# A graph layer on one core: two decoding matmuls for three, the negation and an absolute value on ScalarE, add and relu in one VectorE instruction

## The chip, the core and the metric

The kernel runs on one core of a Trainium2 chip. Its engines are TensorE (PE, with its weight loads as a row of their own, PEld), VectorE (DVE), ScalarE (ACT), GpSimd (POOL) and SyncE (SP); each works through its own queue in order, and they wait for one another by semaphores. The metric is the time of one execution on the device in microseconds (us).

## The reference

One layer of a graph network over N = 6250 nodes with D = 64 features and E = 206250 directed edges, sorted by their target:

```python
h = jnp.maximum(_layernorm(x, axis=-1), 0.0)
msg = jax.nn.relu(h[src] + edge_attr)
agg = jax.ops.segment_sum(msg, dst, num_segments=N)
t = h + agg
out = x + jax.nn.relu(t @ W1 + b1) @ W2 + b2
```

All of it is in float32. The costly part is `h[src]`: a row of 64 numbers for each of 206250 edges.

## The kernel before

**Tiling.** An edge group `g` is 768 edges: 128 partitions with G = 6 edges each. There are 268 groups and a rest. The first five are handled alone in the set-up; the others form KS = 150 sets `k` of one or two groups, and the main loop `for k in range(KS): both_units(k)` handles one set per turn. Its order of work is written out by hand in `both_units`, one half for odd and one for even `k`; generators (`picking`, `decoding`, `compared`, `counted`, `others`) are advanced a step at a time between the other calls, and each engine's queue holds its instructions in that order.

**Two ways to fetch a row of h.** Of a group's six edges per partition, three are gathered by POOL: `gather` (L241) issues an indirect DMA for each column of 128 edges, out of the copy of h in DRAM (`h_rows`) into `xg`. 114 of the sets have two groups and so six such gathers (the last fewer); 36 sets have one group and none. The other three are fetched with matmuls:

- `find` (L594) and `back` (L607): DVE compares lists of source nodes with numbers and writes one-hot matrices `found` and `backs` in float16.
- `across_of` (PE, `half`, L633) picks rows of h with `found`; ACT copies them to `across`; `turn_of` (PE, L644) transposes them into the one bank `turn`; `turn_out` (ACT) copies that to `picked` (L650); `pick` (PE, L655) puts them to the edges' places, and `decode_parts` (ACT, L720) copies the result to `both`.

**Two halves of a number.** A float16 matmul carries 11 bits, so the h of L633 is kept in `hp` as two float16 parts, `hi` and `lo`, scaled by UP = 2^12; the sign of `hi` carries one more bit, which says how the last place is to be corrected (`ln_parts`). After the pick, `decode_minus` (DVE) makes `minus = max(-both, 0)`. `decode_sum` (PE, L734) sums the parts into the PSUM bank `joint` with three matmuls for each of 6 columns of a set: `both` by `join`, `minus` by `weigh_sign` (it undoes the sign) and `minus` by `weigh_last` (the last place). `decode_add` (DVE, L743) adds the scaled sum to the edges' attributes in `ea`, `xg_add` (DVE, L750) adds the gathered rows to the other half of `ea`, and `messages` (ACT, L755) takes the relu of all of it in place.

**Sums.** `one_hot` (DVE, L696) marks for each edge its target in a window of 32 nodes; `window_sum` (PE, L769) multiplies messages by that mark, into `joint` as well, beside the decoded columns; `sum_into_z` (DVE, L687) adds the windows to `z`. At even `k` the windows of sets k-3 and k-2 are summed. Finished blocks of 512 nodes go through `hidden` and `result` and are stored.

**Pace of the gathers.** `passes` counts the nominal PE time of the matmuls as they are written; each time another SPREAD[0] ns (later SPREAD[1]) have been counted, it issues the next of 652 pending gathers, which waits for that matmul. The first 30 of the sets' gathers and 30 of the set-up's are issued ahead of that. `xgs` has room for ten sets, `eas` for four.

Of the kernel before, what the change touches and what calls it, by code (L numbers as in the profile page):

```python
# [9 lines left out]

F32 = mybir.dt.float32
I32 = mybir.dt.int32
I16 = mybir.dt.int16
F16 = mybir.dt.float16
AF = mybir.ActivationFunctionType
ALU = mybir.AluOpType
# [3 lines left out]
N, E, D = 6250, 206250, 64  # L20
P = 128
G = 6
# [19 lines left out]
H = 3  # L42
PP, RR = 128, 49
# [18 lines left out]
GROUPS = []  # L62
g = F0
# [6 lines left out]
KS = len(GROUPS)  # L70
# [6 lines left out]
QW = Q // VERSIONS  # L77
PLACED = [0, 2, 6, 22, 38, NCH]
RING, AHEAD, EAS = 10, 6, 4
SPREAD = 1110, 1190  # L80
UP, FINE = 2.0 ** 12, 2.0 ** 11
HALF_LAST = 2.0 ** -24 * (1 + 2.0 ** -9)
NUDGE, ODD = 0.12 * 2.0 ** -12, 0.35 * 2.0 ** -12
# [5 lines left out]
def kernel(  # L89
# [14 lines left out]
    nc = tc.nc  # L104
    ctx.enter_context(tc.manual_schedule())

    const = ctx.enter_context(tc.tile_pool(name="const", bufs=1))
    work = ctx.enter_context(tc.tile_pool(name="work", bufs=2))
# [14 lines left out]
    def x_rows(r, n):  # L123
        i = r // XH
        return xs[i][:, r - i * XH:r - i * XH + n]
# [34 lines left out]
    ident = lnp.tile([P, P], F32, name="ident", bufs=1)  # L160
# [13 lines left out]
    ones_b = const.tile([P, P], F16, name="ones_b")  # L174
    nc.vector.memset(ones_b, 1.0)
    join = const.tile([P, D], F16, name="join")
    weigh_sign = const.tile([P, D], F16, name="weigh_sign")
    weigh_last = const.tile([P, D], F16, name="weigh_last")
    nc.vector.scalar_tensor_tensor(join, ident[:, :D], FINE, ident[:, D:], op0=ALU.mult, op1=ALU.add)
    for t, by in ((weigh_sign, 2 * FINE), (weigh_last, -FINE * HALF_LAST)):  # L180
        nc.vector.tensor_scalar_mul(t, ident[:, :D], by)
    upper = const.tile([P, P], F16, name="upper")
    nc.gpsimd.affine_select(out=upper, in_=ones_b, compare_op=ALU.is_gt, fill=0.0, base=0,
                            pattern=[[1, P]], channel_multiplier=-1)
# [13 lines left out]
    hp = const.tile([PP, RR, 2, D], F16, name="hp")  # L198
# [8 lines left out]
    eas = [const.tile([P, 2, G, D], F32, name=f"ea{i}") for i in range(EAS)]  # L207
    xgs = [const.tile([P, 2, H, D], F32, name=f"xg{i}") for i in range(RING)]
    RAWS = (F0 + 1) // 2
# [37 lines left out]
    def first_col(g):  # L247
        return 0 if g < NG else G - CT

    def pool_cols(g):  # L250
        return G if g < F0 else 0 if g in WHOLE else G - H
# [20 lines left out]
    pending = [(g, j) for k in range(AHEAD, KS) for g in GROUPS[k] for j in range(first_col(g), pool_cols(g))]  # L272
    gates = [0, SPREAD[0]]
    current = []

    def passes(it, ns):
# [5 lines left out]
        if pending and gates[0] >= gates[1]:  # L282
            gates[1] += SPREAD[k >= 2 * SETS * SINGLES]
            assert k < set_of[pending[0][0]][0] < k + RING, (k, set_of[pending[0][0]][0], gates)
# [171 lines left out]
    joint = psum.tile([P, 512], F32, name="joint", bufs=1)  # L456
# [24 lines left out]
    def ln_rows(r, n, v):  # L481
        h = x_rows(r, n)
        nc.vector.reciprocal(v, v)
        nc.vector.tensor_scalar_mul(v, v, UP)
        nc.vector.scalar_tensor_tensor(h, h, 0.0, v.unsqueeze(2).to_broadcast([PP, n, D]),
                                       op0=ALU.max, op1=ALU.mult)
        nc.sync.dma_start(
            out=h_rows.rearrange("(p r) d -> p r d", r=RR)[:, r:r + n].rearrange("p r d -> p (r d)"),
            in_=h.rearrange("p r d -> p (r d)"),
        )  # L490
        return r, n, h
# [11 lines left out]
    def ln_turned():  # L503
        zv = z[:D, :NP].rearrange("d (p r) -> d p r", r=RR)
        for pt, r, n in turned_rows:
            nc.scalar.activation(zv[:, :, r:r + n], pt[:, :n].rearrange("d u p -> d p u"), AF.Copy, scale=1.0 / UP)
        turned_rows.clear()

    def ln_parts(r, m, h):
        hi, lo = hp[:, r:r + m, 0], hp[:, r:r + m, 1]  # L510
        rest = lnp.tile([PP, m, D], F32, name="rest")
        sign = lnp.tile([PP, m, D], F16, name="sign")
        nc.scalar.copy(hi, h)
        nc.scalar.mul(rest, h, FINE)
        yield
        nc.vector.scalar_tensor_tensor(rest, hi, -FINE, rest, op0=ALU.mult, op1=ALU.add)
        paces.append(nc.vector.scalar_tensor_tensor(lo, hi, NUDGE, rest, op0=ALU.mult, op1=ALU.add))
        yield
        nc.vector.tensor_tensor(rest, lo, rest, ALU.subtract)
        nc.vector.scalar_tensor_tensor(sign, hi, ODD, rest, op0=ALU.mult, op1=ALU.is_lt)  # L520
        yield
        nc.scalar.activation(sign, sign, AF.Copy, bias=1.0, scale=-2.0)
        yield
        nc.vector.tensor_tensor(hi, hi, sign, ALU.mult)

    def add_attr(y, xg, ea):
        nc.vector.scalar_tensor_tensor(y, xg, 1.0 / UP, ea, op0=ALU.mult, op1=ALU.add)

    def combine(xg, ea, n):
        add_attr(xg[:, :n], xg[:, :n], ea[:, :n])  # L530
        nc.scalar.activation(ea[:, :n], xg[:, :n], AF.Relu)
        return ea

    left = const.tile([P, CP], I16, name="left")
# [148 lines left out]
    aggs, hots, msgs = {}, {}, {}  # L683
# [20 lines left out]
    def first_messages(g):  # L704
        ea, xg = ring(eas, g), rows_of(g)
        if g < RAW:
            yield from norm_edges(xg)
            nc.vector.tensor_tensor(ea, ea, xg, ALU.add)
        else:
            add_attr(ea, xg, ea)  # L710
        nc.scalar.activation(ea, ea, AF.Relu)
        msgs[g] = ea
        yield

    fetched = {}
# [5 lines left out]

    def decode_minus(k):
        minus = work.tile([P, 2, H * P], F16, name="minus", bufs=1)
        nc.vector.tensor_scalar(minus, fetched[k], -1.0, 0.0, op0=ALU.mult, op1=ALU.max)  # L724
        fetched[k] = fetched[k], minus

    def decode_sum(k):
        both, minus = fetched.pop(k)
        for i in range(2):
            for j in range(H):  # L730
                to = joint[:, (i * H + j) * D:(i * H + j + 1) * D]
                terms = (both, join), (minus, weigh_sign), (minus, weigh_last)
                for n, (rows, weights) in enumerate(terms):
                    it = nc.tensor.matmul(to, rows[:, i, j * P:(j + 1) * P], weights, start=(n == 0), stop=(n == len(terms) - 1))  # L734
                    passes(it, 29)
                yield

    def decode_add(k):
        n = len(GROUPS[k])
        ea = eas[(k + RAWS) % EAS][:, :n]  # L740
        to = ea[:, :, G - H:] if n == 2 else ea[:, 0].rearrange("p (i j) d -> p i j d", i=2)
        to = to.rearrange("p i j d -> p i (j d)")
        nc.vector.scalar_tensor_tensor(to, joint[:, :2 * H * D].rearrange("p (i s) -> p i s", i=2),  # L743
                                       1.0 / (UP * FINE), to, op0=ALU.mult, op1=ALU.add)

    def xg_add(k):
        if len(GROUPS[k]) == 2:
            ea, xg = eas[(k + RAWS) % EAS], xgs[(k + RAWS) % RING]
            to = ea[:, :, :G - H].rearrange("p g j d -> p g (j d)")
            nc.vector.scalar_tensor_tensor(to, xg.rearrange("p g j d -> p g (j d)"), 1.0 / UP, to, op0=ALU.mult, op1=ALU.add)  # L750

    def messages(k):
        gs = GROUPS[k]
        msg = eas[(k + RAWS) % EAS][:, :len(gs)]
        nc.scalar.activation(msg, msg, AF.Relu)  # L755
        for i, g in enumerate(gs):
            msgs[g] = msg[:, i]

# [107 lines left out]
    def weave(*steps):  # L866

        steps = [step for step in steps if step is not None]
        while steps:
            steps = [step for step in steps if next(step, True) is None]  # L870
# [51 lines left out]
    def joined(k):  # L922
        yield from sums(k - 2)
        yield from sums(k - 1)
        yield from decode_sum(k)
# [3 lines left out]
            attr_set(k + EAS - 2)  # L929

    def joint_out(k):
        decode_add(k)
        yield
        if k > 0 and k % 2:
            yield from adds(k - 2)
            yield from adds(k - 1)
        one_hot(GROUPS[k])
        yield

    def both_units(k):  # L940
        current[:] = [k]
        d, odd = divmod(k, 2)
# [5 lines left out]
        if odd:  # L948
# [17 lines left out]
            next(compared, None)  # L966
            next(picking, None)
            turn_at(3 * k + 7)
            if k > 1:
                messages(k - 2)  # L970
            next(picking, None)
            across_at(3 * k + 9)
            counting(k, source, rank_turn)
# [6 lines left out]
            turn_at(3 * k + 8)  # L980
            next(decoding, None)
            next(decoding, None)
            weave(compared, counted, others)
            if not odd and d + 3 < KD:
                source_load(d + 3)
# [6 lines left out]
        else:  # L992
# [2 lines left out]
            next(compared, None)  # L995
            if k:
                decode_minus(k - 1)
            if k > 1:
                messages(k - 2)
            next(picking, None)  # L1000
            next(picking, None)
            counting(k - 1, rank_count)
# [27 lines left out]
            turn_at(3 * k + 8)  # L1030
            next(decoding, None)
            next(decoding, None)
            next(picking, None)
            if k:
                attrs_behind(k - 1)
# [43 lines left out]
    for r, to in quarters[2:]:  # L1079
        v = ln_var(*heads.pop(0))  # L1080
# [125 lines left out]
    any_left = nc.values_load(flag[0:1, 0:1], min_val=0, max_val=P * N)  # L1206
    xbs[NB] = old_rows(NB)
    decode_minus(KS - 1)
    messages(KS - 2)
    for k in (KS - 2, KS - 1):  # L1210
        for g in groups_of(k):
            starts_for(g)
    weave(joined(KS - 1))
    xg_add(KS - 1)
    weave(joint_out(KS - 1))
    messages(KS - 1)
    weave(sums(KS - 1))
    for g in range(KS - 4, KS - 1):
        behind.extend(groups_of(g))
# [30 lines left out]
    with tc.If(any_left > 0):  # L1250
        nc.gpsimd.iota(wide, pattern=[[1, WB]], base=1, channel_multiplier=0, allow_small_or_imprecise_dtypes=True)
        with tc.For_i(0, NG, 1) as i:
# [4 lines left out]
            ea = eas[0][:, 0]  # L1257
# [5 lines left out]
        ea = eas[0][:, 0]  # L1263
# [48 lines left out]
```

## Time and profile before

| | |
|---|---|
| median of 3 runs | 992.82 us (987.42 to 995.36) |
| the profiled execution | 989.2 us, of which 987.4 us from the first to the last instruction (the span) |
| granted TensorE clock, mean over the span | 0.968 of full speed |
| busy: PE, DVE, ACT, POOL | 905.7, 922.7, 780.2, 749.1 us |
| indirect gathers into xg | 682 |

A row of the groups names the line, engine, operation, what it writes and reads with the shapes, and the count; then the busy time in us and the mean of one in ns; then the idle time of the engine just before, with what ended most of it. A row of the timeline starts with the start and the duration in us, and its square bracket has the idle time ahead of the instruction and its releaser. The end of a matmul is modelled, so what one costs the queue is read from start to start.

### The profile page before, as it was taken

To read this page: it belongs to the slowest core of one execution; us is meant where nothing else is said; L and a number is where in the kernel's file an instruction comes from. 1 tells how busy PE (TensorE), PEld (TensorE's weight loads), DVE (VectorE), ACT (ScalarE), POOL (GpSimd) and SP (SyncE) were. 2 spreads that over 40 slices of the span, in tenths; PEclk is the share of its full clock that TensorE was granted. 3 is DMA by queue.
4 is the path that set the end of the run, shared out by engine and by line. 5 is a ranking of instruction groups with operands and counts; after the bars stand their busy time and mean duration, and the time that the engine had idled before them with its cause. 6 is when DMAs were issued, how large, how long until landed. Compare 5 with 4: busy or idle time off the path is not lost.

```text
span 987.4 us, 35954 instructions
## 1 busy us (share of the span) xinstructions
PE 905.7 (92%) x13996; PEld 728.2 (74%) x13996; DVE 922.7 (93%) x2314; ACT 780.2 (79%) x1623; POOL 749.1 (76%) x727
## 2 busy tenths in 40 slices
PE   2249999999999989999999999999999999999986
PEld 1137777878877778787887777887877787787874
DVE  8898999989999999999999899999999999999975
ACT  6528888878888878888888788887887888888873
POOL 7877777777777777777777777777777777777771
PEclk9559999999999999999999999999999999999998
DMA  7436667666766666776766766766766666676841
GB/s 222 140 100 196 192 230 232 208 226 210 217 218 210 216 216 205 223 240 217 225 215 205 227 215 212 261 202 202 243 214 212 223 217 228 214 234 208 272 146 36
DMA packets 93833, 205.63 MB, mean 208 GB/s; under 512 B 24537, under 2 KB 62042, under 8 KB 93658
## 3 DMA queue, kind: packets, MB, share of 16 engines
q1 hardware_dynamic: 70762, 179.87, 51.1%
q0 software_dynamic: 22784, 23.38, 12.8%
q8 instruction: 112, 1.84, 0.7%
q14 instruction: 63, 0.52, 0.2%
q10 hardware_dynamic: 112, 0.03, 0.0%
HBM read 199.07 MB, written 4.13 MB: 206 GB/s over the span
## 4 chain that ended last, share of the span: by engine, by line
PE 60%; DVE 19%; DMA 12%; issue 3%; ACT 3%; DVEq 1%; POOL 1%; SPq 0%; ACTq 0%; POOLq 0%
PE pick L655 19%; PE half L633 13%; DMA xg<-h_rows,src_sb 9%; PE joint L769 8%; PE turn L644 7%; DVE backs L611 6%; PE joint L734 6%; DMA sources<-source_row 2%; PE rows L432 2%; DVE ea L743 2%; DVE found L601 2%; ACT ea L755 2%; PE rows L366 1%; PE half L628 1%; PE rows L808 1%
## 5 line engine op out<-in xcount | busy, mean ns | idle before, releaser
L241 POOL DMA_INDIRECT xg<-h_rows,src_sb x682 | 711.5, 1043 | 207.9 <-issue 52.7
L655 PE MATMUL pick<-backs,picked 128*128 128x384 f16 x1800 | 437.4, 328 | 0.0
L650 ACT COPY picked<-turn 128x512 f16<-128x512 f16 x450 | 262.6, 584 | 69.2 <-PE turn L644 62.0
L639 ACT CAST across<-half 128x512 f16<-128x512 f32 x450 | 264.9, 589 | 18.6 <-PE half L633 10.5
L633 PE MATMUL half<-found,hp 128*128 128x128 f16 x3600 | 276.5, 220 | 0.0
L611 DVE TENSOR_SCALAR backs<-spots,ids 128x1536 f16<-128x1536 int16 x450 | 275.4, 647 | 0.0
L633 PEld LDWEIGHTS <-hp 128*128 128x128 f16 x3600 | 234.5, 98 | 37.9 <-issue 0.6
L601 DVE TENSOR_SCALAR found<-sources,nodes_of 128x1536 f16<-128x1536 int16 x300 | 191.8, 672 | 1.1 <-issue 0.8
L655 PEld LDWEIGHTS <-picked 128*128 128x128 f16 x1800 | 157.3, 99 | 34.0 <-issue 0.3
L644 PE MATMUL turn<-ident_h,across 128*128 128x128 f16 x1800 | 175.8, 220 | 1.7 <-ACT picked L650 1.7
L755 ACT ACTIVATE ea<-ea 128x768 f32<-128x768 f32 x150 | 115.6, 770 | 55.0 <-DVE ea L743 50.5
L644 PEld LDWEIGHTS <-across 128*128 128x128 f16 x1800 | 123.0, 98 | 38.8 <-issue 6.0
L720 ACT CAST both<-pick 128x384 f16<-128x384 f32 x300 | 146.0, 487 | 3.2 <-PE pick L655 3.2
L769 PEld LDWEIGHTS joint<-oh,ea 128*64 128x64 f32 x3176 | 101.2, 138 | 48.9 <-DVE ea L743 24.6
L769 PE MATMUL joint<-oh,ea 128*64 128x32 f32 x3176 | 112.5, 224 | 20.3 <-DVE ea L743 11.6
L734 PE MATMUL joint<-join,both 128*128 128x64 f16 x900 | 127.0, 194 | 0.0
L734 PE MATMUL joint<-weigh_sign,minus 128*128 128x64 f16 x900 | 126.5, 194 | 0.6 <-DVE minus L724 0.5
L734 PE MATMUL joint<-weigh_last,minus 128*128 128x64 f16 x900 | 126.4, 194 | 0.0
L734 PEld LDWEIGHTS <-minus 128*128 128x128 f16 x1800 | 96.9, 98 | 16.5 <-DVE minus L724 1.3
L743 DVE SCALAR_TENSOR_TENSOR ea<-joint,ea 128x384 f32<-128x384 f32 x150 | 82.0, 547 | 22.5 <-PE joint L734 21.7
L734 PEld LDWEIGHTS <-both 128*128 128x128 f16 x900 | 88.1, 99 | 1.7
L696 DVE TENSOR_TENSOR oh<-slot,slots 128x384 f32<-128x384 int16 (+1 forms) x151 | 76.1, 504 | 0.1
(131 smaller groups left out, 777.0 us busy)
## 6 DMA issues: line engine op xcount, KB each, us to landing
sources<-source_row SPq DMA_DIRECT2D x75, 768.0 KB
spots<-spot_rows SPq DMA_DIRECT2D x75, 768.0 KB
ea<-in_edge_attr_dram SPq DMA_DIRECT2D x112, 384.0 KB
xg<-h_rows,src_sb POOLq DMA_INDIRECT x682
ea<-in_edge_attr_dram SPq DMA_DIRECT2D x44, 192.0 KB
xb<-in_x_dram SPq DMA_DIRECT2D x12, 128.0 KB
out_dram<-o SPq DMA_DIRECT2D x12, 128.0 KB
h_rows<-x SPq DMA_DIRECT2D x3, 384.0 KB
```

Source lines behind the costliest of these rows:

```text
L241: it = nc.gpsimd.indirect_dma_start(out=xg[:, j, :], out_offset=None, in_=rows[:, :], in_offset=bass.IndirectOffsetOnAxis(ap=idx[:, j:j + ...
L601: nc.vector.tensor_scalar(found[d][:, b * PARTS + m:b * PARTS + m + PARTS // 2].rearrange("p m u s -> p (m u s)"), sources[d][:, m * 4 * S ...
L611: nc.vector.tensor_scalar(backs[2 * d + u // 2][:, q].rearrange("p u v e -> p (u v e)"), spots[d].bitcast(I16)[:, u * VERSIONS * H * P:(u ...
L633: last = nc.tensor.matmul(ps[:, j * P:(j + 1) * P], hp[:, b * PARTS + m].rearrange("p t d -> p (t d)"), found[d][:, b * PARTS + m].rearran ...
L639: nc.scalar.copy(across[d, q].rearrange("p u j s -> p j u s"), ps.rearrange("p (j u s) -> p j u s", j=J, u=4))
L644: passes(nc.tensor.transpose(ps[:, u * P:(u + 1) * P], ac[:, u].rearrange("p j s -> p (j s)"), ident_h), 56)
L650: nc.scalar.copy(picked[d][:, q].rearrange("p u d -> p (u d)"), turned.pop((d, q)))
L655: it = nc.tensor.matmul(pick_banks[(2 * k + i) % 3][:, :H * P], picked[d][:, q, u], backs[k][:, q // VERSIONS, i, q % VERSIONS, :], start= ...
L720: nc.scalar.copy(fetched[k][:, i], pick_banks[(2 * k + i) % 3][:, :H * P])
L734: it = nc.tensor.matmul(to, rows[:, i, j * P:(j + 1) * P], weights, start=(n == 0), stop=(n == len(terms) - 1))
L755: nc.scalar.activation(msg, msg, AF.Relu)
L769: last = nc.tensor.matmul(pa[i * D:(i + 1) * D], msg[:, j, :], oh[:, j, :], start=(j < lo + 2), stop=(j >= G - 2))
```

## The change

- The sign that `hi` carried now stands on both parts (`ln_parts` multiplies `hi` and `lo` together). The decoded sum then is the wanted number with that sign, and its absolute value is taken. `weigh_sign` and its matmul go: two matmuls for each column, not three.
- `decode_minus` moves from DVE to ACT, as a relu of the negated `both`.
- `decode_out`, new, takes the absolute value on ACT, out of `joint` into a new SBUF tile `exact`; it stands behind the last step of `decoding`.
- `messages` moves from ACT to DVE and to the place of `decode_add`: one instruction adds `exact` and `ea` and takes the relu (`TENSOR_ADD_SAT`, the sum clamped between 0 and infinity). `xg_add` and the first groups' `combine` use the same instruction, so each half of `ea` gets its relu with its add.
- The rows of h in DRAM are no longer scaled by UP; the scaling moves into the copies that make `hi` and `rest`.
- SPREAD goes from 1110 and 1190 to 1074 and 1151.

```diff
-SPREAD = 1110, 1190
+SPREAD = 1074, 1151
...
-    for t, by in ((weigh_sign, 2 * FINE), (weigh_last, -FINE * HALF_LAST)):
-        nc.vector.tensor_scalar_mul(t, ident[:, :D], by)
+    nc.vector.tensor_scalar_mul(weigh_last, ident[:, :D], FINE * HALF_LAST)
...
     def ln_rows(r, n, v):
         nc.vector.reciprocal(v, v)
-        nc.vector.tensor_scalar_mul(v, v, UP)
...
     def ln_parts(r, m, h):
-        nc.scalar.copy(hi, h)
-        nc.scalar.mul(rest, h, FINE)
+        nc.scalar.mul(hi, h, UP)
+        nc.scalar.mul(rest, h, UP * FINE)
...
-        nc.vector.tensor_tensor(hi, hi, sign, ALU.mult)
+        both = hp[:, r:r + m]
+        nc.vector.tensor_tensor(both, both, sign.unsqueeze(2).to_broadcast([PP, m, 2, D]), ALU.mult)
...
+    def add_relu(ea, xg):
+        nc.vector._custom_dve(TENSOR_ADD_SAT, out=ea, in0=xg, in1=ea, s0=float("inf"), s1=0.0)
...
     def decode_minus(k):
-        nc.vector.tensor_scalar(minus, fetched[k], -1.0, 0.0, op0=ALU.mult, op1=ALU.max)
+        nc.scalar.activation(minus, fetched[k], AF.Relu, scale=-1.0)
...
-                terms = (both, join), (minus, weigh_sign), (minus, weigh_last)
+                terms = (both, join), (minus, weigh_last)
...
-    def decode_add(k):
-        n = len(GROUPS[k])
-        ea = eas[(k + RAWS) % EAS][:, :n]
-        to = ea[:, :, G - H:] if n == 2 else ea[:, 0].rearrange("p (i j) d -> p i j d", i=2)
-        to = to.rearrange("p i j d -> p i (j d)")
-        nc.vector.scalar_tensor_tensor(to, joint[:, :2 * H * D].rearrange("p (i s) -> p i s", i=2),
-                                       1.0 / (UP * FINE), to, op0=ALU.mult, op1=ALU.add)
+    def decode_out(k):
+        exact[k] = work.tile([P, 2, H * D], F32, name="exact", bufs=2)
+        nc.scalar.activation(exact[k].rearrange("p i s -> p (i s)"), joint[:, :2 * H * D], AF.Abs, scale=1.0 / (UP * FINE))
...
     def xg_add(k):
-            nc.vector.scalar_tensor_tensor(to, xg.rearrange("p g j d -> p g (j d)"), 1.0 / UP, to, op0=ALU.mult, op1=ALU.add)
+            add_relu(ea[:, :, :G - H].rearrange("p g j d -> p g (j d)"), xg.rearrange("p g j d -> p g (j d)"))
...
     def messages(k):
         msg = eas[(k + RAWS) % EAS][:, :len(gs)]
-        nc.scalar.activation(msg, msg, AF.Relu)
+        to = msg[:, :, G - H:] if len(gs) == 2 else msg[:, 0].rearrange("p (i j) d -> p i j d", i=2)
+        add_relu(to.rearrange("p i j d -> p i (j d)"), exact.pop(k))
...
     def joint_out(k):
-        decode_add(k)
+        messages(k)
...
     def both_units(k):
             turn_at(3 * k + 7)
-            if k > 1:
-                messages(k - 2)
...
             turn_at(3 * k + 8)
             next(decoding, None)
             next(decoding, None)
+            decode_out(k - 1)
```

The last two edits stand in the half for odd `k`; the half for even `k` has the same two, with the old `messages(k - 2)` behind `decode_minus(k - 1)`. Behind the loop, the last set's calls change in the same way.

More of the change, by code (lines that the diff above doesn't have):

```diff
@@ L9 @@
 from concourse._compat import with_exitstack
+from concourse.dve_ops import TENSOR_ADD_SAT
 F32 = mybir.dt.float32
@@ L176 @@
     join = const.tile([P, D], F16, name="join")
-    weigh_sign = const.tile([P, D], F16, name="weigh_sign")
     weigh_last = const.tile([P, D], F16, name="weigh_last")
     nc.vector.scalar_tensor_tensor(join, ident[:, :D], FINE, ident[:, D:], op0=ALU.mult, op1=ALU.add)
-    for t, by in ((weigh_sign, 2 * FINE), (weigh_last, -FINE * HALF_LAST)):
-        nc.vector.tensor_scalar_mul(t, ident[:, :D], by)
+    nc.vector.tensor_scalar_mul(weigh_last, ident[:, :D], FINE * HALF_LAST)
     upper = const.tile([P, P], F16, name="upper")
@@ L505, in ln_turned @@
         for pt, r, n in turned_rows:
-            nc.scalar.activation(zv[:, :, r:r + n], pt[:, :n].rearrange("d u p -> d p u"), AF.Copy, scale=1.0 / UP)
+            nc.scalar.copy(zv[:, :, r:r + n], pt[:, :n].rearrange("d u p -> d p u"))
         turned_rows.clear()
@@ L523, in ln_parts @@
         yield
-        nc.vector.tensor_tensor(hi, hi, sign, ALU.mult)
-    def add_attr(y, xg, ea):
-        nc.vector.scalar_tensor_tensor(y, xg, 1.0 / UP, ea, op0=ALU.mult, op1=ALU.add)
+        both = hp[:, r:r + m]
+        nc.vector.tensor_tensor(both, both, sign.unsqueeze(2).to_broadcast([PP, m, 2, D]), ALU.mult)
+    def add_relu(ea, xg):
+        nc.vector._custom_dve(TENSOR_ADD_SAT, out=ea, in0=xg, in1=ea, s0=float("inf"), s1=0.0)
     def combine(xg, ea, n):
-        add_attr(xg[:, :n], xg[:, :n], ea[:, :n])
-        nc.scalar.activation(ea[:, :n], xg[:, :n], AF.Relu)
+        add_relu(ea[:, :n].rearrange("p j d -> p (j d)"), xg[:, :n].rearrange("p j d -> p (j d)"))
         return ea
@@ L707, in first_messages @@
             yield from norm_edges(xg)
[L708 to L712, printed above, removed]
+        msgs[g] = combine(xg, ea, G)
         yield
@@ L736, in decode_sum @@
                 yield
-    def decode_add(k):
-        n = len(GROUPS[k])
-        ea = eas[(k + RAWS) % EAS][:, :n]
-        to = ea[:, :, G - H:] if n == 2 else ea[:, 0].rearrange("p (i j) d -> p i j d", i=2)
-        to = to.rearrange("p i j d -> p i (j d)")
-        nc.vector.scalar_tensor_tensor(to, joint[:, :2 * H * D].rearrange("p (i s) -> p i s", i=2),
-                                       1.0 / (UP * FINE), to, op0=ALU.mult, op1=ALU.add)
+    exact = {}
+    def decode_out(k):
+        exact[k] = work.tile([P, 2, H * D], F32, name="exact", bufs=2)
+        nc.scalar.activation(exact[k].rearrange("p i s -> p (i s)"), joint[:, :2 * H * D], AF.Abs, scale=1.0 / (UP * FINE))
     def xg_add(k):
@@ L748, in xg_add @@
             ea, xg = eas[(k + RAWS) % EAS], xgs[(k + RAWS) % RING]
-            to = ea[:, :, :G - H].rearrange("p g j d -> p g (j d)")
-            nc.vector.scalar_tensor_tensor(to, xg.rearrange("p g j d -> p g (j d)"), 1.0 / UP, to, op0=ALU.mult, op1=ALU.add)
+            add_relu(ea[:, :, :G - H].rearrange("p g j d -> p g (j d)"), xg.rearrange("p g j d -> p g (j d)"))
     def messages(k):
@@ L997, in both_units @@
                 decode_minus(k - 1)
-            if k > 1:
-                messages(k - 2)
             next(picking, None)
@@ L1032, in both_units @@
             next(decoding, None)
+            if k:
+                decode_out(k - 1)
             next(picking, None)
@@ L1208 @@
     decode_minus(KS - 1)
-    messages(KS - 2)
     for k in (KS - 2, KS - 1):
@@ L1213 @@
     weave(joined(KS - 1))
+    decode_out(KS - 1)
     xg_add(KS - 1)
     weave(joint_out(KS - 1))
-    messages(KS - 1)
     weave(sums(KS - 1))
```

## The prediction

> **What bounds the kernel now.** I began with the busy times, since the change takes work from PE and DVE and gives some to ACT, and then looked for the engine that never waits. In the page's list of engines and in its groups (count, busy us, mean ns, idle before):
>
> ```profile
> PE 905.7 (92%) x13996; PEld 728.2 (74%) x13996; DVE 922.7 (93%) x2314; ACT 780.2 (79%) x1623; POOL 749.1 (76%) x727
> L241 POOL DMA_INDIRECT xg<-h_rows,src_sb x682 | 711.5, 1043 | 207.9 <-issue 52.7
> ```
>
> By the shares PE and DVE are full and POOL has a quarter to spare. The second row contradicts that: 207.9 us of idle over 682 gathers is 0.305 us before each. The source view of L241 (min/median/max ns, first and last start) and the timeline of POOL late and early show that this 0.305 is no wait:
>
> ```profile
> L241 POOL DMA_INDIRECT xg<-h_rows,src_sb x682: 940/945/2602, 47.8 to 966.0; - x171
> L750 DVE SCALAR_TENSOR_TENSOR ea<-xg,ea x114: 543/548/598, 81.3 to 974.7; 128x384 f32<-128x384 f32 x114
> ...
> 87.06 0.94 POOL L241 DMA_INDIRECT xg<-h_rows,src_sb  x1 [0.30 <-PE half L628]
> ...
> 962.12 0.94 POOL L241 DMA_INDIRECT xg<-h_rows,src_sb  x1 [0.30 <-PE half L633]
> 963.37 1.03 POOL L241 DMA_INDIRECT xg<-h_rows,src_sb  x1 [0.30 <-PE pick L655]
> 964.71 0.94 POOL L241 DMA_INDIRECT xg<-h_rows,src_sb  x1 [0.30 <-DMA xg<-h_rows,src_sb]
> 965.96 0.94 POOL L241 DMA_INDIRECT xg<-h_rows,src_sb  x1 [0.30 <-DMA xg<-h_rows,src_sb]
> ```
>
> Every gather begins 0.30 us after the one before, whatever is named as its releaser. From 47.8 to 966.0 that is 918.2 / 681 = 1.348 us each, which is the mean of 1.043 plus 0.305. POOL is full from end to end; the PE pace points (`passes`) have gone by when it gets there.
>
> What uses the gathered rows is `xg_add` (L750). Its first use, at 81.3, comes about 27 us after set 0's sixth gather (47.8 + 5 x 1.31, the early period being (87.06 - 47.8) / 30). The last use, at 974.7, starts 8.7 us after the last gather (966.0). So POOL lost 18 us of lead over the kernel. How much of the 8.7 is needed is in the chain of waits (start, us):
>
> ```profile
> 504.29 2.30 DMA xg<-h_rows,src_sb
> 506.59 0.54 DVE ea L750
> ```
>
> A gather's rows land 2.30 us after its start. **The profiled execution was thus bound by PE and DVE, with 8.7 - 2.3 = 6.4 us left before POOL takes over.** That it is PE that sets the pace of the rest, the groups and the waits say:
>
> ```profile
> L734 PE MATMUL joint<-weigh_sign,minus 128*128 128x64 f16 x900 | 126.5, 194 | 0.6 <-DVE minus L724 0.5
> ...
> ACT picked L650 <- PE turn L644: 62.0, 164, 1.8
> PEld joint L769 <- DVE ea L743: 24.6, 35, 2.6
> DVE ea L743 <- PE joint L734: 21.7, 27, 5.3
> ```
>
> ACT waits for PE, and PE waits for hardly anything but the window sums.
>
> **What decides a gather's length.** 682 x (1043 - 940) ns = 70 us is the excess over its shortest form, and it is the one quantity by which POOL can become faster or slower. Pairs from the timeline, DVE instruction and gather:
>
> ```profile
> 121.36 0.55 DVE L750 SCALAR_TENSOR_TENSOR ea<-xg,ea 128x384 f32<-128x384 f32 x1
> 121.50 1.34 POOL L241 DMA_INDIRECT xg<-h_rows,src_sb  x1 [0.30 <-DVE oh L696]
> ...
> 913.87 0.55 DVE L750 SCALAR_TENSOR_TENSOR ea<-xg,ea 128x384 f32<-128x384 f32 x1
> 914.10 1.25 POOL L241 DMA_INDIRECT xg<-h_rows,src_sb  x1 [0.30 <-DVE oh L696]
> ...
> 228.44 0.56 DVE L743 SCALAR_TENSOR_TENSOR ea<-joint,ea 128x384 f32<-128x384 f32 x1 [0.28 <-PE joint L734]
> 228.69 0.94 POOL L241 DMA_INDIRECT xg<-h_rows,src_sb  x1 [0.30 <-PE joint L734]
> ...
> 853.70 0.56 DVE L743 SCALAR_TENSOR_TENSOR ea<-joint,ea 128x384 f32<-128x384 f32 x1 [1.06 <-PE joint L734]
> 853.77 0.94 POOL L241 DMA_INDIRECT xg<-h_rows,src_sb  x1 [0.30 <-PE joint L734]
> ```
>
> Where `xg_add` (both inputs in SBUF) starts inside the 0.30 us gap, the gather behind it is longer by what is left of the DVE instruction: 36 of its 114 do so (first and last pair above), 0.31 us each. The old decoding add L743 (one input in PSUM) started there 3 times in 150 (first and last above) and delayed nothing. Two more kinds matter here, again first and last pair (the gather of the last `minus` is the one of 963.37 above):
>
> ```profile
> 102.85 0.54 DVE L696 TENSOR_TENSOR oh<-slot,slots 128x384 f32<-128x384 int16 x1
> 102.90 1.31 POOL L241 DMA_INDIRECT xg<-h_rows,src_sb  x1 [0.30 <-issue]
> ...
> 955.19 0.54 DVE L696 TENSOR_TENSOR oh<-slot,slots 128x384 f32<-128x384 int16 x1
> 955.39 1.43 POOL L241 DMA_INDIRECT xg<-h_rows,src_sb  x1 [0.30 <-DMA xg<-h_rows,src_sb]
> ...
> 161.98 0.35 DVE L724 TENSOR_SCALAR minus<-both 128x768 f16<-128x768 f16 x1
> 162.03 1.10 POOL L241 DMA_INDIRECT xg<-h_rows,src_sb  x1 [0.30 <-PE pick L655]
> ...
> 963.23 0.35 DVE L724 TENSOR_SCALAR minus<-both 128x768 f16<-128x768 f16 x1
> ```
>
> The one-hot does it 64 times in 150 at 0.30 us (19 us in all), `minus` 22 times at 0.115 us (2.5 us).
>
> The Trainium skill, "SBUF — State Buffer", section "SBUF: two separate sides", says that VectorE and GpSimd share one port pair as an exclusive lock, taken also by a VectorE operation with two SBUF inputs against a GpSimd operation that reads SBUF, and that the loser blocks. The pairs above agree for L750 and L696 (0.31 and 0.30 us) and for L743 by its absence. The rule speaks against this change, which turns L743 into an operation with two SBUF inputs; what that could cost is the slower rival below.
>
> **The change part by part.**
>
> *PE.* 6 of 18 decoding matmuls go from each of 150 sets: 900. They cost their pace and not their 194 ns; one trio's first matmul and the next trio's first:
>
> ```profile
> 504.72 0.19 PE L734 MATMUL joint<-join,both 128*128 128x64 f16 x1
> ...
> 504.80 0.19 PE L734 MATMUL joint<-join,both 128*128 128x64 f16 x1
> ```
>
> 80 ns for three is 27 ns each: 900 x 27 = 24 us off PE. That alone would make 989.2 - 24 = 965.
>
> *DVE and ACT.* The rows for what goes and comes:
>
> ```profile
> L724 DVE TENSOR_SCALAR minus<-both 128x768 f16<-128x768 f16 x150 | 54.1, 361 | 2.9 <-ACT both L720 2.9
> L743 DVE SCALAR_TENSOR_TENSOR ea<-joint,ea 128x384 f32<-128x384 f32 x150 | 82.0, 547 | 22.5 <-PE joint L734 21.7 <-PE turn L644 0.7
> L755 ACT ACTIVATE ea<-ea 128x768 f32<-128x768 f32 x114 | 96.5, 847 | 52.0 <-DVE ea L743 48.0 <-DVE backs L611 3.8
> L755 ACT ACTIVATE ea<-ea 128x384 f32<-128x384 f32 x36 | 19.0, 528 | 3.0 <-DVE ea L743 2.5 <-issue 0.2
> L720 ACT CAST both<-pick 128x384 f16<-128x384 f32 x300 | 146.0, 487 | 3.2 <-PE pick L655 3.2
> L522 ACT ACTIVATE sign<-sign 128x768 f16<-128x768 f16 x3 | 2.4, 828 | 0.0
> L485 DVE SCALAR_TENSOR_TENSOR x<-x,ln_v 128x768 f32<-128x768 f32 x3 | 2.9, 958 | 0.1
> ```
>
> DVE loses `minus` (54 us) and L743 (82 us) and gets 150 of the new add-with-relu over 384 elements; the 114 of `xg_add` change to it as well. The trace has no such operation. I take the 0.55 us of L750, same shape and operands. Above, 0.96 us (L485, as if it went twice over its data) would put 264 x 0.41 = 108 us on an engine with 65 us idle; below, 0.36 us (L724) would save 50 us that POOL doesn't let through. So DVE comes to about 869 us.
>
> ACT loses the relu (115 us) and gets 150 negations at 828 ns (124 us, L522) and 150 absolute values from PSUM at 487 ns (73 us, L720): plus 82, to 862 us. The cover is ACT's 207 us of idle, 62 of them ahead of `picked`. Without it, PE would wait at the next `turn`, whose one bank `picked` empties. Behind the wait of the new `decode_out` stand the copies `both` and `across`; `messages` on DVE waits for it. `minus` waits for ACT itself only. That `messages` ends earlier than the relu did takes away up to 24.6 us of PE waits, off the end as long as POOL sets it.
>
> *Set-up and gates.* The scale by UP, the doubled sign product and the merged first messages are a dozen instructions of under 0.96 us (L485 is the longest kind there), some gone and some doubled, under POOL's unbroken queue: nothing, at most 1 us if the stores of `h_rows` come earlier. SPREAD shrinks by 3.2% with the matmuls; POOL is behind its gates anyway: nothing.
>
> **The sum.** PE wants to gain another 24 us on POOL, besides the 18. Of 27 us of lead 2.3 have to stay, so it is used up after 24.7 / 42 = 59% of the way, and from there POOL sets the pace. Span: 987.4 - 6.4 = 981.0. Then what changes in the gathers' excess:
> - `minus` off DVE: -2.5.
> - `messages` with two SBUF inputs: the decoding add came into the gap 3 times in 150, since it follows comparisons that fall in with POOL; but after an idle DVE the start is anywhere. I take 50 such starts (27 today behind PE, more behind the longer way over ACT), 0.30 / 1.35 of them in the gap, 0.31 each: +3.4. Bounds: 0, and 19.2 as the one-hot.
> - `xg_add` when it waits for its rows: 2.30 us after a gather's start the next has begun (1.25) and ended (2.19) and the one after begins at 2.49, so it starts right in the gap. 41% of 114 = 47 at 0.31 is 14.6; landings scatter, half: +7.3.
>
> 981.0 - 2.5 + 3.4 + 7.3 = 989.2, and with the 1.8 us around the span **991 us**, against 989.2 for the profiled execution. That one lies 3.6 us under the median of 992.82; I leave 991 as the time. A measurement of this kernel tells no less than 1% from no change (its runs spread over 0.8%).
>
> **The rivals.**
> 1. *POOL becomes lighter: faster.* If the new operation doesn't delay gathers, `xg_add`'s 11.3 us (36 x 0.31) go too: 981.0 - 11.3 - 2.5 = 967.2, and 969 in time, just above the 965 of PE alone. For: it is another kind of operation. Against: it reads the same two SBUF tensors. A mere shift in phase against POOL could do as much. Chance 0.24.
> 2. *`messages` blocks POOL: slower.* Place: the end of each set, ahead of the one-hot. If it meets gathers as the one-hot does, it costs 64 x 0.30 = 19.2 instead of 3.4: 1007 us. It decides from 16 us of added excess, some 52 gathers more (999.1 is 1% over). For: L696's row; against: L743's 3 in 150. Chance 0.14.
> 3. *ACT or a long new operation* sets the pace: at 0.96 us DVE would hold 977 us of work, with today's 65 us of idle 1042. Slower, 0.07.
> 4. *It doesn't do what it says*: the matmuls go but the clock or the waits eat them; 989, inside the forecast.
>
> **Numbers.** Forecast 0.55, nearly all within 1%; faster 0.25 with the edge of the forecast, slower 0.21, same 0.54. The range takes in rivals 1 and 2: 967 to 1007.
>
> **What would show it.** Gathers still 0.30 us apart with a mean between 1.03 and 1.07 us; last gather within 10 us of 966; the use of the last rows 2 to 4 us behind it; DVE waiting for xg's DMA, which no row of the waits has now; fewer than 20 us of PE waits at the window sums. A mean under 1.02 us means rival 1, over 1.08 rival 2; gaps above 0.31 between gathers would end the argument.

## The result, and the profile after

The changed kernel takes **981.54 us** (median of 20 runs, 979.77 to 984.59), the kernel before 992.01 beside it: a ratio of 0.9909, 95% interval [0.9896, 0.9922], or 0.9% less. One of the 20 runs of the kernel before took 2324 us, the others 986.59 to 995.36. The forecast was 991, its range 967 to 1007. The profiled execution took 982.09 us, its span is 980.4, 7.0 less than before. So 900 matmuls, 24 us of PE by the forecast's sum, brought 7.

The list of engines and the groups of the changed kernel, the last four rows from the view that keeps shapes apart:

```profile
PE 888.0 (91%) x13096; PEld 702.0 (72%) x13096; DVE 885.5 (90%) x2159; ACT 829.3 (85%) x1768; POOL 742.9 (76%) x727
L240 POOL DMA_INDIRECT xg<-h_rows,src_sb x682 | 704.8, 1034 | 207.9 <-issue 61.0
L718 ACT ACTIVATE minus<-both 128x768 f16<-128x768 f16 x150 | 129.0, 860 | 2.4
...
L736 ACT ACTIVATE exact<-joint 128x384 f32<-128x384 f32 x150 | 74.6, 497 | 2.9 <-PE joint L728 2.9
...
L526 DVE CUSTOM_DVE_ANT_1 ea<-exact,ea 128x384 f32<-128x384 f32 x114 | 63.3, 555 | 31.2 <-ACT exact L736 31.0
L526 DVE CUSTOM_DVE_ANT_1 ea<-xg,ea 128x384 f32<-128x384 f32 x114 | 62.8, 551 | 17.2 <-DMA xg<-h_rows,src_sb 8.4 <-DMA source_row<-source 6.1 <-issue 2.7
L526 DVE CUSTOM_DVE_ANT_0 ea<-exact,ea 128x384 f32<-128x384 f32 x36 | 20.1, 559 | 17.4 <-ACT exact L736 17.1
L694 DVE TENSOR_TENSOR oh<-slot,slots 128x384 f32<-128x384 int16 x114 | 62.5, 548 | 0.1
```

The source view of the gathers' line in the changed kernel, and, from the groups of the kernel before, the row of `xg_add` for comparison:

```profile
L240 POOL DMA_INDIRECT xg<-h_rows,src_sb x682: 940/945/2646, 48.3 to 959.7; - x171
```

```profile
L750 DVE SCALAR_TENSOR_TENSOR ea<-xg,ea 128x384 f32<-128x384 f32 x114 | 62.7, 550 | 0.5 <-issue 0.5
```

The gathers still have 207.9 us of gaps, 0.305 each: POOL is as full as it was, and its last gather starts 6.3 us earlier only because a gather's mean fell from 1043 to 1034 ns. The row to see is that of `xg_add`: VectorE sat idle for **17.2 us ahead of it, where it was 0.5**. The names behind that idle (a source row, "issue") are those of whatever came last by the profile. One of these waits in the timeline of VectorE and of POOL, and the same moment in the chain of the changed kernel:

```profile
650.87 0.55 DVE L694 TENSOR_TENSOR oh<-slot,slots 128x384 f32<-128x384 int16 x1
654.98 0.56 DVE L526 CUSTOM_DVE_ANT_1 ea<-xg,ea 128x384 f32<-128x384 f32 x1 [3.56 <-DMA xg<-h_rows,src_sb]
```

```profile
648.76 1.16 POOL L240 DMA_INDIRECT xg<-h_rows,src_sb  x1 [0.30 <-issue]
...
652.72 0.95 POOL L240 DMA_INDIRECT xg<-h_rows,src_sb  x1 [0.30 <-PE joint L728]
```

```profile
652.72 2.28 DMA xg<-h_rows,src_sb
655.00 0.54 DVE ea L526
```

The chain names the gather of 652.72, but that can't be the one that VectorE waited for. This is the 75th `xg_add`; each set has six gathers, so its own are the 445th to 450th, and the gather of 652.72 is the 453rd, of the next set. The last of its own is the one of 648.76. The trace also keeps when the transfers of a gather report that they have ended; about 5% of the reports are missing. By them the rows of 648.76 landed at 654.73, 5.97 us after the gather's start, and the add, which VectorE could have begun at 651.4, began 0.25 us later. Twelve of the 114 adds wait longer than 0.15 us. Ten of them begin 0.1 to 0.3 us after the last rows of their own set have landed; the other two waits are of 0.24 and 0.28 us. In the kernel before no set's rows landed later than 1.35 us ahead of its add. So the rows are what is late. The stretches of the two kernels say when this sets in. The bounds are the starts of `both` of sets 0, 50 and 125 (us, then each engine's busy time, the granted clock, DMA share, GB/s); before:

```profile
82.00:385.00 303.00, 294.98 (x4588) 237.82 (x4587) 287.63 (x718) 248.38 (x524) 234.25 (x226) 0.99 0.67 216
...
385.00:832.00 447.00, 438.61 (x6921) 354.33 (x6919) 429.18 (x1076) 371.29 (x785) 346.50 (x330) 1.00 0.68 220
```

and after:

```profile
81.00:373.00 292.00, 285.28 (x4279) 226.77 (x4276) 272.28 (x668) 264.25 (x574) 225.86 (x218) 1.00 0.68 222
...
373.00:822.00 449.00, 433.27 (x6494) 343.74 (x6491) 412.54 (x1001) 398.46 (x863) 346.92 (x336) 1.00 0.68 220
```

The first 50 sets are 11 us faster, the next 75 are 2 us slower, although PE has 5.3 us less to do in them: PE's idle there grows from 8.4 to 15.7 us. The lighter kernel ran ahead until it had caught up with POOL (the first add that waits for its rows starts at 431.2), and then went at POOL's pace.

### The profile page after: what moved, and what is told of

It reads as the page before. It is cut to its first block, busy times and chain, and to the rows that moved or that the text cites. A ratio compares the mean times of both kernels' runs of the same rounds, so it can differ in the third digit from the quotient of the medians.

```text
span 980.4 us, 33848 instructions
## 1 busy us (share of the span) xinstructions
PE 888.0 (91%) x13096; PEld 702.0 (72%) x13096; DVE 885.5 (90%) x2159; ACT 829.3 (85%) x1768; POOL 742.9 (76%) x727
## 4 chain that ended last, share of the span: by engine, by line
PE 54%; DVE 15%; ACT 10%; DMA 7%; issue 6%; POOL 6%; DVEq 1%; POOLq 0%; SPq 0%; ACTq 0%
PE pick L653 15%; PE half L631 12%; PE joint L761 9%; PE turn L642 8%; DVE backs L609 7%; DMA xg<-h_rows,src_sb 6%; ACT picked L648 4%; POOL xr L240 4%; PE joint L728 4%; DVE ea L526 3%; ACT across L637 2%; ACT minus L718 2%; POOL xg L240 2%; PE rows L431 2%; ACT exact L736 2%
## 5 line engine op out<-in xcount | busy, mean ns | idle before, releaser
L240 POOL DMA_INDIRECT xg<-h_rows,src_sb x682 | 704.8, 1034 | 207.9 <-issue 61.0
L648 ACT COPY picked<-turn 128x512 f16<-128x512 f16 x450 | 269.2, 598 | 66.7 <-PE turn L642 61.3
L637 ACT CAST across<-half 128x512 f16<-128x512 f32 x450 | 271.6, 604 | 12.8 <-PE half L631 9.0
L761 PEld LDWEIGHTS joint<-oh,ea 128*64 128x64 f32 x3176 | 102.6, 138 | 45.7 <-DVE oh L694 18.0
L761 PE MATMUL joint<-oh,ea 128*64 128x32 f32 x3176 | 115.4, 224 | 17.4 <-DVE oh L694 14.4
L718 ACT ACTIVATE minus<-both 128x768 f16<-128x768 f16 x150 | 129.0, 860 | 2.4
L728 PE MATMUL joint<-weigh_last,minus 128*128 128x64 f16 x900 | 112.5, 193 | 0.0
L728 PE MATMUL joint<-join,both 128*128 128x64 f16 x900 | 112.5, 193 | 0.0
L526 DVE CUSTOM_DVE_ANT_1 ea<-exact,ea 128x384 f32<-128x384 f32 x114 | 63.3, 555 | 31.2 <-ACT exact L736 31.0
L728 PEld LDWEIGHTS <-minus 128*128 128x128 f16 x900 | 69.9, 98 | 14.6
L526 DVE CUSTOM_DVE_ANT_1 ea<-xg,ea 128x384 f32<-128x384 f32 x114 | 62.8, 551 | 17.2 <-DMA xg<-h_rows,src_sb 8.4
L736 ACT ACTIVATE exact<-joint 128x384 f32<-128x384 f32 x150 | 74.6, 497 | 2.9 <-PE joint L728 2.9
```

The lines of the kernel that those rows point to most:

```text
L240: it = nc.gpsimd.indirect_dma_start(out=xg[:, j, :], out_offset=None, in_=rows[:, :], in_offset=bass.IndirectOffsetOnAxis(ap=idx[:, j:j + ...
L526: nc.vector._custom_dve(TENSOR_ADD_SAT, out=ea, in0=xg, in1=ea, s0=float("inf"), s1=0.0)
L637: nc.scalar.copy(across[d, q].rearrange("p u j s -> p j u s"), ps.rearrange("p (j u s) -> p j u s", j=J, u=4))
L648: nc.scalar.copy(picked[d][:, q].rearrange("p u d -> p (u d)"), turned.pop((d, q)))
L761: last = nc.tensor.matmul(pa[i * D:(i + 1) * D], msg[:, j, :], oh[:, j, :], start=(j < lo + 2), stop=(j >= G - 2))
```

## The experiments

Two theories stood after the result. **A**: POOL's stream of gathers sets the pace once the lead is used up. **B**: the new wait does it, VectorE for the absolute value. For B speaks a row of the waits of the changed kernel (us, times, longest):

```profile
DVE ea L526 <- ACT exact L736: 48.1, 42, 6.3
```

**1. The changed kernel with 164 of the 682 gathers into `xg` left out.** Their columns keep old rows.

```diff
-            gather(rows_of(g)[:, j:], src_sb[:, g * G + j:], 1, h_rows, [it])
+            if set_of[g][0] < 40 or j < 2:
+                gather(rows_of(g)[:, j:], src_sb[:, g * G + j:], 1, h_rows, [it])
```

> The changed kernel with two of six gathers left out from set 40 on, once more (in the first run of it the kernel before took 1227 us on that chip, against 992 in the result, with gaps of over 1 us between gathers). Theory A (POOL sets the end of the changed kernel): where the kernel before takes 992, 960 to 970 us, a ratio of 0.968 to 0.978. Theory B (the wait for ACT's absolute value sets it): 977 to 983 us, 0.985 to 0.991 as with all gathers.

It took 965.21 us, the kernel before 991.85 beside it: 0.9752 [0.9715, 0.9788]. Its groups, waits and stretches (same sets as above):

```profile
L240 POOL DMA_INDIRECT xg<-h_rows,src_sb x518 | 555.2, 1072 | 320.6 <-PE pick L654 92.1
```

```profile
L527 DVE CUSTOM_DVE_ANT_1 ea<-xg,ea 128x384 f32<-128x384 f32 x114 | 62.7, 550 | 0.5 <-DMA xg<-h_rows,src_sb 0.2 <-issue 0.2
```

```profile
DVE ea L527 <- ACT exact L737: 56.0, 47, 4.6
```

```profile
81.00:374.00 293.00, 286.12 (x4300) 227.47 (x4299) 272.87 (x671) 264.88 (x575) 221.91 (x212) 1.00 0.68 222
...
374.00:810.00 436.00, 429.19 (x6472) 341.65 (x6470) 399.45 (x999) 397.39 (x862) 244.83 (x223) 1.00 0.66 217
```

POOL now waits for its points of pace on PE, the idle ahead of `xg_add` is 0.5 us again, and 16 us are gone, while the wait of B has even grown, from 48.1 to 56.0 us. B falls as an account of these 16 us: a wait that grows while the time shrinks did not hold them. With fewer gathers VectorE's busy time also falls, from 412.5 to 399.5 us in the 75 sets, and that could be the gain as well. Against it stand the first 50 sets: there POOL has nearly as much to do (212 instructions against 218), the lead is still there, and the changed kernel needs 292 us and this one 293, 5.85 us a set. That is the pace that this kernel keeps later with fewer gathers (436 / 75 = 5.81) and the changed kernel doesn't (449 / 75 = 5.99). The sets are not quite alike: the kernel before took 303 / 50 = 6.06 and 447 / 75 = 5.96 us for the same ones. The kernel before with fewer gathers was not run on a chip where it takes 992 us, so what they cost that kernel stays open.

**2. The one-hot and `messages` with one input in PSUM.** `slots` is copied into free columns of the bank of `turn`, and the absolute value stays in `joint`. It tests the rule by which a gather grows.

```diff
+    slots_ps = turn_bank[:, 256:256 + W]
+    nc.vector.tensor_copy(slots_ps, slots)
...
-            slots.unsqueeze(1).to_broadcast([P, n, W]), ALU.is_equal)
+            slots_ps.unsqueeze(1).to_broadcast([P, n, W]), ALU.is_equal)
...
-        nc.scalar.activation(exact[k].rearrange("p i s -> p (i s)"), joint[:, :2 * H * D], AF.Abs, scale=1.0 / (UP * FINE))
+        nc.scalar.activation(joint[:, :2 * H * D], joint[:, :2 * H * D], AF.Abs, scale=1.0 / (UP * FINE))
```

> The changed kernel with two operands moved from SBUF to PSUM: the constant `slots` of the one-hot into the unused half of the turn bank, and the absolute value written back in place into `joint`, from where `messages` reads it. No instruction more in the loop. Theory A, with VectorE operations of two SBUF inputs delaying gathers: the 12 us of one-hot delays and 2 us of `messages` delays go, the mean gather falls from 1034 to about 1015 ns, the time to 966 to 973 us (0.974 to 0.981). Theory B, or if the delays hang on something else than the operands' home: gathers at 1034 ns, 980 to 985 us.

It took 1093.1 us, 1.1041 [1.0999, 1.1083]. The time is lost to something else (below), but the gathers can still be read. First and last pair of one-hot and gather, of `messages` and gather, and of `xg_add` and gather in its timeline:

```profile
103.01 0.54 DVE L696 TENSOR_TENSOR oh<-slot,turn 128x384 f32<-128x384 int16 x1
103.07 0.95 POOL L240 DMA_INDIRECT xg<-h_rows,src_sb  x1 [0.31 <-DMA xg<-h_rows,src_sb]
...
1046.14 0.54 DVE L696 TENSOR_TENSOR oh<-slot,turn 128x384 f32<-128x384 int16 x1
1046.35 0.94 POOL L240 DMA_INDIRECT xg<-h_rows,src_sb  x1 [0.30 <-issue]
...
129.39 0.56 DVE L528 CUSTOM_DVE_ANT_1 ea<-joint,ea 128x384 f32<-128x384 f32 x1 [0.91 <-ACT joint L737]
129.65 0.94 POOL L240 DMA_INDIRECT xg<-h_rows,src_sb  x1 [0.30 <-PE rows L363]
...
1031.94 0.56 DVE L528 CUSTOM_DVE_ANT_1 ea<-joint,ea 128x384 f32<-128x384 f32 x1 [0.53 <-ACT joint L737]
1032.06 0.95 POOL L240 DMA_INDIRECT xg<-h_rows,src_sb  x1 [0.30 <-issue]
...
110.67 0.55 DVE L528 CUSTOM_DVE_ANT_1 ea<-xg,ea 128x384 f32<-128x384 f32 x1
110.77 1.26 POOL L240 DMA_INDIRECT xg<-h_rows,src_sb  x1 [0.30 <-issue]
...
953.89 0.55 DVE L528 CUSTOM_DVE_ANT_1 ea<-xg,ea 128x384 f32<-128x384 f32 x1
954.10 1.25 POOL L240 DMA_INDIRECT xg<-h_rows,src_sb  x1 [0.30 <-issue]
```

36 one-hots and 25 `messages` start in the gap ahead of a gather here, and the 61 gathers together are 0.5 us over their shortest form; 13 `xg_add`, still with both inputs in SBUF, lengthen theirs by 0.36 us each. In the changed kernel 43 one-hots cost 12.0 us. So for these two operations it is the second SBUF input that delays a gather. The Trainium skill states such a rule in "SBUF — State Buffer", section "SBUF: two separate sides", and this trace agrees with it (0.5 us in 61 starts). It is not the only way to a longer gather: `minus`, with one input, delayed 22 of them in the kernel before. The waits show what the edit cost:

```profile
DVE ea L528 <- ACT joint L737: 180.5, 100, 5.6
...
PE turn L644 <- DVE oh L696: 71.5, 80, 2.2
...
PEld L644 <- DVE oh L696: 38.4, 46, 1.1
```

The matmuls into `turn` now wait for the one-hot that reads other columns of the same bank: in this program the order of accesses is kept for the bank as a whole.

**3. The other runs.** They ran on chips on which the kernel before takes 1227 to 1231 us, and were to separate PE from POOL and to find a better order.

The kernel before and the changed one with the gathers left out as in 1:

> The kernel before, with two of the six gathers left out for each two-group set from set 40 on (those columns keep old rows; some 165 gathers, 220 us of POOL). Theory A (POOL's gathers set the end after the change; before it, PE and DVE did with a few us to spare): no gain beyond the few us by which the gathers were tight at some sets, 985 to 992 us. Theory B (the chain PE, ACT, DVE sets the end in both kernels, POOL only follows its gates): 992, unchanged. This run is the base for the next one.

> The changed kernel with the same gathers left out. Theory A: POOL no longer holds the kernel, so the 24 us of matmuls come through: 960 to 970 us. Theory B (the wait for the absolute value on ACT, 48 us of DVE idle, eats the matmuls' gain): 977 to 983 us, as with all gathers.

> The kernel before with two of six gathers left out from set 40 on, where the kernel before takes about 992. Theory A: PE and DVE set the end of the kernel before with 1 to 6 us to spare, so 985 to 992 us, ratio 0.993 to 1.0; together with the 965 us of the changed kernel under the same edit that is the whole change's worth without POOL, 20 to 27 us. Theory B: 992. If it falls by over 10 us, POOL was already the bound before the change, and my 6.4 us of lead were wrong.

The kernel before with the two matmuls alone, and with fewer gathers besides:

```diff
-SPREAD = 1110, 1190
+SPREAD = 1074, 1151
...
-                terms = (both, join), (minus, weigh_sign), (minus, weigh_last)
+                terms = (both, join), (minus, weigh_last)
```

> The kernel before with the weigh_sign matmul left out (so the decoded rows have the wrong sign in part) and the new SPREAD, nothing else of the change. Theory A: PE is 24 us shorter, but POOL lets through only what its lead allows and what its gathers gain by chance: 980 to 987 us, as the whole change. Theory B: with relu and absolute value where they were, the matmuls' gain comes through: 965 to 970 us.

> The two matmuls of the run before this one and the fewer gathers together, in the kernel before. Theory A: 963 to 970 us, the whole 24 us below the run with fewer gathers alone. Theory B: the same as with all gathers, 965 to 970 us. If it is far above 970, PE isn't what the matmuls make shorter, and DVE is the bound behind POOL.

> The kernel before with the weigh_sign matmul left out and the new SPREAD (decoded rows wrong in sign), where the kernel before takes about 992. Theory A (POOL lets through only its lead of a few us and what its gathers gain by chance): 982 to 988 us, ratio 0.990 to 0.996. Theory B (PE sets the end, and only the new waits of the whole change keep its gain from showing): 965 to 970 us, 0.973 to 0.978.

> The kernel before with the middle one of its three decoding matmuls left out (900 of 13996, about 24 us of PE at 27 ns each) and SPREAD as in the changed kernel; VectorE and ScalarE work as before. The sum loses its sign correction, so it computes other values at the places where the sign mattered. Theory A (POOL's stream sets the pace once PE is lighter): on a chip where the kernel before takes about 992 us, only what is left of the lead and the excess of the gathers can move: 982 to 990 us, with the gathers still 0.30 us apart for the whole run. Theory B (PE sets the pace): 992 less 24, 966 to 971 us. If the kernel before takes 1220 us or more on the chip of this run: A and the earlier runs say 0.995 to 1.0, B 0.98.

The changed kernel with `xg_add` one step later (the half for odd `k`; the other half in the same way), and without the pass over the absolute value:

```diff
-            xg_add(k - 1)
...
             next(compared, None)
+            xg_add(k - 1)
```

> The changed kernel with xg_add moved behind the first comparison of the next unit, on DVE alone; same instructions, same results. A VectorE instruction that follows a comparison hardly ever starts in the 0.3 us between two gathers, one that follows the one-hot often does (41 of 114 xg_add). Theory A: most of the 11 us of xg_add's delays go, gathers at 1018 to 1026 ns, 970 to 977 us (ratio 0.978 to 0.985). Theory B, or a wrong reading of the phase: gathers at 1030 to 1040 ns, 980 to 984 us.

> The changed kernel with the add of the gathered rows moved behind the next step of the comparisons, in both halves of the loop; the same operations, one place later in VectorE's queue. Theory A (POOL's gathers set the pace, and a VectorE operation with two SBUF inputs lengthens a gather where it starts in the 0.30 us between two): the rows are wanted about 1 us later, so the lead lasts longer, and the adds no longer stand directly behind messages; if fewer of the 41 of 114 that start in a gap do so, up to 11 us go: 970 to 980 us, and where the comparisons take the add's place in the gaps, no change, 979 to 984. Theory B (the new wait for the absolute value sets the pace): the wait comes first as before, 979 to 984 us. If the kernel before takes 1220 us or more on the chip of this run: 0.99 to 1.0 by either.

```diff
-        exact[k] = work.tile([P, 2, H * D], F32, name="exact", bufs=2)
-        nc.scalar.activation(exact[k].rearrange("p i s -> p (i s)"), joint[:, :2 * H * D], AF.Abs, scale=1.0 / (UP * FINE))
+        exact[k] = joint[:, :2 * H * D].rearrange("p (i s) -> p i s", i=2)
```

> The changed kernel without the absolute value (sign and scale of the decoded part stay wrong): `messages` adds `joint` from PSUM straight away, so ACT does 75 us less and DVE doesn't wait for ACT (48 us of idle in the changed kernel). Theory A: POOL still sets the end; the 2 us of gather delays behind `messages` may go: 976 to 982 us, ratio 0.985 to 0.990. Theory B (that wait is what eats the matmuls' gain): 960 to 970 us, 0.968 to 0.978.

| run | us | ratio to the kernel before |
|---|---|---|
| before, fewer gathers | 1076.95; again 1094.84 (1076.08, 1080.6, 1109.09, 1112.29) | 0.8767 [0.8724, 0.881]; none given |
| after, fewer gathers | 1072.1 | 0.8725 [0.867, 0.8779] |
| before, two matmuls | 1225.04; 1226.15; 1226.77 | 0.998 [0.9951, 1.001]; 0.997 [0.9942, 0.9998]; 0.9968 [0.9931, 1.0005] |
| before, two matmuls, fewer gathers | 1073.51 | 0.8746 [0.8695, 0.8798] |
| after, `xg_add` later | 1222.52; 1225.25 | 0.9945 [0.9909, 0.9982]; 0.9967 [0.9932, 1.0003] |
| after, no absolute value | 1218.03 | 0.9891 [0.9818, 0.9963] |

The runs with fewer gathers lie where neither theory put them: A had 0.993 to 1.0 for the kernel before and 0.968 to 0.978 for the changed one, and all came to 0.87. For a chip where the kernel before takes 992 us, a fall of over 10 us in it was to mean that POOL was its bound before the change; here it fell by 12%, and what it does where it takes 992 stays open. The runs with two matmuls come to 0.997 to 0.998, near where A had them (0.990 to 1.0), but they don't speak for A. In the third of them the row of `xg_add` shows no wait, POOL waits for PE, and PE's weight loads wait too; the last row is that of the same loads in the kernel before where it takes 992 us:

```profile
L750 DVE SCALAR_TENSOR_TENSOR ea<-xg,ea 128x384 f32<-128x384 f32 x114 | 62.9, 551 | 0.5 <-issue 0.5
```

```profile
PEld L644 <- issue: 106.7, 191, 2.5
...
POOL xg L241 <- PE pick L655: 88.6, 101, 2.8
...
PEld joint L769 <- issue: 72.8, 152, 3.5
```

```profile
PEld L644 <- issue: 6.0, 16, 0.5
```

In this run PE stands still for reasons that the profile doesn't show, and the gathered rows are there in time. The granted clock was 0.940 here and 0.968 in the kernel before where it takes 992 us, 3% apart where the times are 24% apart. 164 gathers less take 12% off, so the gathers have to do with it; how, no run tells. What can be read there is a caution: with fewer gathers, PE's lighter work brought next to nothing either (1076.95 to 1072.1, the intervals overlap). The stretches of the same 75 sets, of the kernel before and of the changed one, both with fewer gathers:

```profile
468.00:920.00 452.00, 443.69 (x6920) 356.43 (x6917) 418.37 (x1077) 366.75 (x785) 240.18 (x223) 1.00 0.64 209
```

```profile
465.00:914.00 449.00, 433.27 (x6490) 343.29 (x6487) 399.77 (x1001) 400.54 (x863) 249.67 (x224) 1.00 0.64 212
```

Of 10.4 us of PE 3 arrive. That the matmuls' 24 us come through with fewer gathers is thus seen only where the kernel before takes 992 us (989.2 - 24 = 965 by the forecast's sum, 965.21 in experiment 1; against the 991.85 beside it that is 26.6 less), and there beside whatever the missing gathers give by themselves. The later `xg_add` and the version without the absolute value cannot be judged here: the changed kernel itself was not run on these chips.

## Why the prediction was right, and where it was not

**Right: POOL is full.** Gaps of 0.305 us on 76% busy, as before; the last gather at 959.7, within the 10 us of 966; the mean of 1034 ns within 1.03 to 1.07 us. VectorE now waits for the rows. PE's 24 us became 7; the 17 us that VectorE sat ahead of `xg_add` are as much as is missing, though no run ties the two wait by wait.

**Wrong: the lead, -6.4 us.** I read it from the last set alone: 8.7 us between the last gather and its use, less 2.3. Both steps fail. The 2.30 us came from the chain, which names a gather of a later set here too: the add of 506.59 is the 55th, its rows had landed by 493.8, and the gather of 504.29 is the 341st. By the reports, rows land 2.3 us after the start of their gather at the soonest, 4.2 at the median and about 8 at the latest, in both kernels. And the lead is not smallest in the last set: in the kernel before the closest rows landed 1.35 us ahead of their add, that of 949.1. So some 1.35 us were left, not 6.4. In the changed kernel the lead was used up at 431.2, after 44% of the span where the sum had 59%, and the twelve waits come in bursts, the long ones at 501 and 510, 655, 791 and 800, 928 and 942: some 145 us apart. At the end there is lead again, and the use of the last rows is 7.4 us behind the last gather (967.1 - 959.7), not 2 to 4. From the last gather to the end of the span the kernel needed 21.4 us (987.4 - 966.0) before and 20.7 now: this term was worth -0.7.

**Wrong: the one-hot, 0.** It was left as it was. Its starts in the gap fell from 64 to 43, its cost from 19.2 to 12.0 us: -7.2, the largest term there is. The forecast names it in a half sentence ("a mere shift in phase against POOL could do as much") and gives it no size. Why the new order meets the gaps less often, no run shows.

**Too large: `messages`, +3.4, and `xg_add`, +7.3.** First and last pair of `messages` in the gap, in the timeline of the changed kernel:

```profile
141.38 0.56 DVE L526 CUSTOM_DVE_ANT_1 ea<-exact,ea 128x384 f32<-128x384 f32 x1 [0.94 <-ACT exact L736]
141.60 1.15 POOL L240 DMA_INDIRECT xg<-h_rows,src_sb  x1 [0.31 <-issue]
...
891.00 0.56 DVE L526 CUSTOM_DVE_ANT_1 ea<-exact,ea 128x384 f32<-128x384 f32 x1 [0.95 <-ACT exact L736]
891.22 1.15 POOL L240 DMA_INDIRECT xg<-h_rows,src_sb  x1 [0.30 <-issue]
```

11 of 150 at 0.20 us are +2.2: the kind of start was right, 50 starts on an idle VectorE were 42 (the count of the wait above). Another 13 start within 0.004 us of a gather's own start and delay nothing. `xg_add` came into the gap 41 times (11.2 us) instead of 36 (11.3): no change. I had 47 of them starting in the gap once they wait for their rows, with a phase worked out from the 2.30 us; only ten waited for rows, because the lead ran out at single sets and not for good.

**Right: `minus`, -2.5.** It left VectorE, and its delays with it. Together: -2.5 + 2.2 - 7.2 - 0.1 makes -7.6; all 712 gathers, those of the set-up included, lost 6.2 us of excess over 940 ns (77.2 to 71.0), so the comparisons and the rest gave 1.4 back. 6.2 and 0.7 are the span's 7.0, to rounding. So the mechanism held, that the end moves by what the gathers lose. That lead would be won at the end was wrong in kind. That the forecast missed by no more than 1% is in part luck: it had the gathers' excess 14.4 us too high (+8.2 where it was -6.2) and the lead 5.7 us too large, and the two errors went opposite ways.

**Not as foretold: the window sums.** PE was to wait less than 20 us for them. The wait of 24.6 us for `ea` is gone, but one for the one-hot, which was 5.4, has come in its place, and the idle ahead of these weight loads fell only from 48.9 to 45.7 us:

```profile
PEld joint L761 <- DVE oh L694: 18.0, 30, 1.8
```

**The rivals.** The first (a lighter POOL) happened in part, by phase. The second fell at 11 of 150. The third fell twice: the new operation takes 0.555 us where 0.55 was taken, and ACT came to 829 us instead of 862, since its instructions overlap when they follow one another (their durations add up to 981.7 us). DVE came to 885.5 instead of 869 us; with POOL setting the end, that row of the sum did not count.

## What to carry to other kernels

A queue can be full at 76% busy: equal gaps in front of every instruction, whatever is named as releaser, are part of the instruction's price. Before a saving on another engine is counted, compare when each product of that queue lands with when it is used, for every set and not for the last alone; the saving ends where the smallest of these leads ends. The name that a chain of waits gives to a transfer is a guess where several share a semaphore; count which transfer the instruction really needs. What lengthens such a queue's instructions by chance of phase can move the time as much as the change that one is pricing.

## What the runs showed of the hardware

- An indirect gather is lengthened by a VectorE instruction with two inputs in SBUF that starts in the 0.30 us gap ahead of it (before: 36 `xg_add` at 0.31 us, 64 one-hots at 0.30); with one input in PSUM, 61 starts there cost 0.5 us in all.
- The rows of an indirect gather of 128 rows land 2.3 us after its start at the soonest, 4.2 at the median and about 8 at the latest (the 682 gathers into `xg`, in both kernels).
- The new add with relu on VectorE takes 551 to 559 ns for 128x384, as the two-input add did (547 to 550).
- On some chips the kernel before takes 24% longer (1227 to 1231 us). With two decoding matmuls for three it has 106.7 us of idle on "issue" there ahead of one line's weight loads; the kernel before had 6.0 where it takes 992. Leaving out 164 gathers took 12% off the kernel before on such chips, and 1.7% off the changed kernel where the kernel before takes 992 (981.54 to 965.21).
